# A graph network on one core: a look woven into a projection, attention's sums added a step later, and the ends of loops reordered

## The chip, the cores and the metric

The kernel runs on one core of a Trainium2 chip. The metric is the device time of one execution in microseconds (us), median of several runs. TensorE is called PE below, VectorE DVE, ScalarE ACT, GpSimd POOL and SyncE SP, as in the profile.

## What is computed

There are 3125 nodes with 256 features and 53,125 edges sorted by their destination. Two attention layers of four heads come first, then a row norm, then three relational layers, then a row norm again:

```python
# attention layer, twice
q, k, v = x@wq+bq, x@wk+bk, x@wv+bv          # 4 heads of 64
alpha = sum(q[dst]*k[src], -1)/sqrt(64)
ex = exp(alpha - segment_max(alpha, dst)[dst])
out = segment_sum(v[src]*ex/segment_sum(ex, dst)[dst], dst) + x@ws + bs
x = leaky_relu(batch_norm(out))              # over all nodes, slope 0.1
...
x = layernorm(x0 + x)
# relational layer, three times
msg = relu(x[src]*(edge_attr@nn_w.T + nn_b))
x = x@root + bias + sum_r mean_over_edges_of_type_r(msg, dst)@W[r]
...
x = layernorm(x_attention + x)
```

## The kernel before

**Tiles.** The edges are 416 tiles of 128, in 52 groups of 8. Nodes are 25 blocks of 128 for attention and 25 blocks of 126 (3 x 42) for the relational part.

**Look and first projection** (`gnn_kernel`, L171 to L359). Three rows of indices (dst, src, edge type) and x are loaded, SP issuing the rows and ACT the x pieces of eight blocks. The look turns the rows into columns, checks on the chip that the windows hold, and makes offsets and masks: some 90 small DVE instructions with small PE transposes between them. The projection takes two node blocks at a time: PE turns each block (L354), ACT copies it to `xT` (L355), PE multiplies by the keys' and values' weights (L383; four matmuls for two blocks, which the trace counts as eight), DVE adds the bias (L390, L393), SP writes to the table `kv_tab` (L396). Here a scheduler of the framework chooses the order on each engine; everywhere after it the order is that of the code. A branch on a checked flag follows.

**Attention** (`window_attention`). Each step `it` of a loop handles several groups in different stages. `rows(it+2)` has POOL issue eight indirect DMAs (L408), each gathering one tile's rows of keys and values from `kv_tab` into one of six `kvg` buffers. `queries` and `logits` (L487, L492, L494) handle group `it`; `turn` (L499) group it-1; `maxima` (L504, L505) group it-2; `weigh` (L511 to L522) forms the exponentials of group it-2 on ACT and scales its 8 x 4 value blocks by 32 ACT instructions of 65 columns; `nodes_of` (L527) makes eight one-hot tiles of group it-3 on DVE; `sums` (L534) multiplies them with the weighted values of group it-4, which frees its `kvg` buffer; `add` (L545) adds the result to an accumulator. The PSUM tile of `sums`, `pof`, has one buffer. When a block's last group has been added, `finish` divides (L564 to L567), PE adds the skip product (L572, L574), ACT moves it to `xT` (L578), DVE takes statistics (L583). The loop runs four steps past the last group, in the same order, with half the scaling on DVE (L522). `norm` then makes the batch norm's scale `sc` (L591 to L597).

**Between the layers.** After layer one, `normalise` (ACT L603, DVE L604) and the second projection alternate by two blocks (L383 again, weights of layer two), and the next gathers wait for the table. After layer two, seven steps of up to four 126-row blocks: normalise the next step's columns, `back` (PE turns a block and adds x by a second matmul with the identity, L727, L729), row statistics on DVE (L743, L744), square root on ACT (L746), reciprocal and shift on DVE (L747, L748), four scaling instructions on ACT (L751), and a write to `h_tab` (L753), from which the next gathers read.

**Relational layers** (`window_relational`). 104 half groups; POOL gathers from `h_tab` (L408, into `xsf`), PE makes edge weights (`ewf`, L824), DVE and ACT the messages (L842, L843), PE sums by one-hots (`ppf`, L850), DVE adds to a ring `kacc` three half groups later (L864). A node block, once complete, passes through `means` (DVE L878), two `turn`s (PE L889, L890; ACT L891, L893), `product` (PE L900; eight matmuls, which the trace counts as sixteen), `total` (DVE L905) and, in the last layer, `norm` (L919, L920); one of them per half group. For the last two blocks (23 and 24) what is left runs after the loop, ordered by stage: all turns first, then the products, then the totals. The next layer's gathers wait for the last write to `h_tab` (L907).

Of the kernel before, what the change touches and what calls it, by code (L numbers as in the profile page):

```python
# [8 lines left out]
F32 = mybir.dt.float32  # L9
# [15 lines left out]
H = 4  # L25
# [111 lines left out]
def gnn_kernel(ctx: ExitStack, tc: tile.TileContext, A, out):  # L137
# [33 lines left out]
    with tc.tile_pool(name="lk", bufs=1) as sp, tc.tile_pool(name="lkw", bufs=2) as wp, \  # L171
            tc.tile_pool(name="lkps", bufs=1, space=PSUM) as ps, \
            tc.tile_pool(name="lkps2", bufs=2, space=PSUM) as ps2:
        x = sp.tile([P, NT, D], F32, name="xf")
        V.memset(x[:, NT - 1, :], 0.0)
        for i in range(0, NT - 1, 8):
            S.dma_start(x[:, i:i + 8, :], A["x"][i * P:(i + 8) * P, :].rearrange("(i p) c -> p i c", p=P))
        S.dma_start(x[:NL, NT - 1, :], A["x"][(NT - 1) * P:, :])
        rows = {}
        for name in ("dst", "src", "edge_type_3"):  # L180
            t = sp.tile([RB, B, P], I32, name=name + "_r")
            if name == "dst":
                GP.iota(t[:, B - 1, :].rearrange("r (a c) -> r a c", c=32), pattern=[[1, 4], [0, 32]], base=N,
                        channel_multiplier=0)
            else:
                V.memset(t[:, B - 1, :], 0)
            a = A[name]
            n = (B - 1) * RB * P
            SY.dma_start(t[:, :B - 1, :], a[:n].rearrange("(b r c) -> r b c", b=B - 1, c=P))
            SY.dma_start(t[:TF - (B - 1) * RB, B - 1, :], a[n:TF * P].rearrange("(r c) -> r c", c=P))  # L190
            SY.dma_start(t[TF - (B - 1) * RB:, B - 1, :TR], a[TF * P:].unsqueeze(0))
            rows[name] = t
        w, bias = kv_weights(tc, A, 1, sp)

# [4 lines left out]


        d = sp.tile([RB, B, P], F32, name="d_f")
        V.tensor_copy(d, rows["dst"])
        ends = sp.tile([1, 2, T], F32, name="ends")
        for e in range(2):
            t = ps.tile([P, T], F32, name="smallps")[:1, :]
            for b in range(B):
                TE.transpose(t[:, b * RB:(b + 1) * RB], d[:, b, e * (P - 1):e * (P - 1) + 1], ident[:RB, :RB])
            V.tensor_copy(ends[:, e, :], t)
        first, last = ends[:, 0, :], ends[:, 1, :]
        halves = sp.tile([64, 2, T], F32, name="halves")  # L210
        for e in range(2):
            t = ps2.tile([P, T], F32, name="colf")
            for b in range(B):
                TE.transpose(t[:64, b * RB:(b + 1) * RB], d[:, b, e * 64:(e + 1) * 64], ident[:RB, :RB])
            V.tensor_copy(halves[:, e, :], t[:64, :])

# [3 lines left out]
        v = sp.tile([RB, B, P], F32, name="v")  # L220
        V.tensor_tensor(v[:, :, :P - 1], d[:, :, :P - 1], d[:, :, 1:], op=OP.subtract)
        V.tensor_reduce(worst[:RB, 0:1], v[:, :, :P - 1], AX.XY, OP.max)
        c = sp.tile([64, T], F32, name="c64")
        V.tensor_tensor(c, halves[:, 0, :], halves[:, 1, :], op=OP.subtract)
        V.tensor_reduce(worst[:64, 1:2], c, AX.X, OP.max)
        V.tensor_tensor(c[:, :T - 1], halves[:, 1, :T - 1], halves[:, 0, 1:], op=OP.subtract)
        V.tensor_reduce(worst[:64, 2:3], c[:, :T - 1], AX.X, OP.max)
        V.tensor_scalar(worst[:, 1:], worst[:, 1:], 1.0, None, op0=OP.add)
        wt = ps.tile([P, T], F32, name="smallps")[:3, :P]
        TE.transpose(wt, worst, ident)  # L230
        w1 = sp.tile([3, 1], F32, name="w1")
        V.tensor_reduce(w1, wt, AX.X, OP.max)
        wu = ps.tile([P, T], F32, name="smallps")[:1, :3]
        TE.transpose(wu, w1, ident[:3, :3])

        bad = sp.tile([1, 6], F32, name="bad")
        V.tensor_reduce(bad[:, 0:1], wu, AX.X, OP.max)
        r1 = sp.tile([1, T], F32, name="r1")
        for i, (tiles, width) in enumerate(((2, W2), (4, KN), (G, P))):
            n = T // tiles  # L240
            V.tensor_tensor(r1[:, :n], last[:, tiles - 1::tiles], first[:, ::tiles], op=OP.subtract)
            V.tensor_scalar(r1[:, :n], r1[:, :n], -float(width - 1), None, op0=OP.add)
            V.tensor_reduce(bad[:, 1 + i:2 + i], r1[:, :n], AX.X, OP.max)
# [4 lines left out]
        V.tensor_tensor(ahead, first[:, G::G], ahead, op=OP.subtract)  # L248
        V.tensor_reduce(bad[:, 5:6], ahead, AX.X, OP.max)
# [5 lines left out]
        V.tensor_tensor(need, need, first[:, G::G], op=OP.subtract)  # L255
        V.tensor_reduce(bad[:, 4:5], need, AX.X, OP.max)
# [3 lines left out]
        V.tensor_tensor(lim, first[:, ::2], lim, op=OP.subtract)  # L260
        b1 = sp.tile([1, 2], F32, name="b1")
        V.tensor_reduce(b1[:, 0:1], lim, AX.X, OP.max)
        V.tensor_reduce(b1[:, 1:2], bad, AX.X, OP.max)
        V.tensor_tensor(b1[:, 0:1], b1[:, 0:1], b1[:, 1:2], op=OP.max)
        V.tensor_single_scalar(flag, b1[:, 0:1], 0.0, op=OP.is_le)


        pairs = sp.tile([1, 2, T], F32, name="pairs")
        V.tensor_copy(pairs[:, 0, :].rearrange("o (a k) -> o a k", k=2), bc(first[:, ::2], 2, 2))
        V.memset(pairs[:, 1, 0:1], 0.0)  # L270
        V.tensor_tensor(pairs[:, 1, 1:], first[:, 1:], last[:, :T - 1], op=OP.is_equal)
        tr = ps.tile([P, T], F32, name="smallps")[:RB, :2 * B].rearrange("r (k b) -> r k b", k=2)
        for k in range(2):
            for b in range(B):
                TE.matmul(tr[:, k, b:b + 1], pairs[:, k, b * RB:(b + 1) * RB], ones[:1, :1], start=True, stop=True)
        per = sp.tile([RB, 2, B], F32, name="per")
        V.tensor_copy(per, tr)

        pen = sp.tile([RB, B, P], F32, name="pen")
        V.tensor_tensor(pen[:, :, 1:], d[:, :, 1:], d[:, :, :P - 1], op=OP.is_equal)  # L280
        V.tensor_copy(pen[:, :, 0], per[:, 1, :])
        V.tensor_scalar(pen, pen, -1.0, BIG, op0=OP.add, op1=OP.mult)
        SY.dma_start(pen_d[FP:FP + EP].rearrange("(b r c) -> r b c", b=B, c=P), pen)

        ld = sp.tile([RB, B, P], F32, name="ld")
        V.tensor_tensor(ld, d, bc(per[:, 0, :], 2, P), op=OP.subtract)
        SY.dma_start(ld_d.rearrange("(b r c) -> r b c", b=B, c=P), ld)
        _, dm = floor42(V, sp, d.rearrange("r b c -> r (b c)"), [RB, B * P], "d42")
        kr = sp.tile([RB, B, P], F32, name="kr")
        V.scalar_tensor_tensor(kr, rows["edge_type_3"], float(KN), dm.rearrange("r (b c) -> r b c", b=B),  # L290
                               op0=OP.mult, op1=OP.add)


        s_f = sp.tile([RB, B, P], F32, name="s_f")
        V.tensor_copy(s_f, rows["src"])
        nr = sp.tile([RB, B, P], F32, name="nr")
        V.tensor_single_scalar(rows["dst"], rows["dst"], P - 1, op=OP.bitwise_and)
        V.tensor_copy(nr, rows["dst"])
        for col, u in ((src_c, s_f), (nr_c, nr), (kr_c, kr)):
            t = ps2.tile([P, T], F32, name="colf")  # L300
            for b in range(B):
                TE.transpose(t[:, b * RB:(b + 1) * RB], u[:, b, :], ident[:RB, :RB])
            V.tensor_copy(col, t)


        pid = sp.tile([P, 1], F32, name="pid")
        GP.iota(pid, pattern=[[0, 1]], base=0, channel_multiplier=1, allow_small_or_imprecise_dtypes=True)
        V.tensor_copy(q_row, first[:, ::2])
        ni = sp.tile([1, NG], I32, name="ni")
        V.tensor_single_scalar(ni, q_row[:, ::4], 7, op=OP.logical_shift_right)  # L310
        nf = sp.tile([1, NG], F32, name="nf")
        V.tensor_copy(nf, ni)
        V.tensor_scalar(g_off, nf, float(AC), None, op0=OP.mult)
        lo = sp.tile([1, NG], F32, name="lo")
        V.scalar_tensor_tensor(lo, nf, -float(P), first[:, ::G], op0=OP.mult, op1=OP.add)
        kq, km = floor42(V, sp, first[:, ::4], [1, Q4], "n42")
        kn = sp.tile([1, 2, Q4], F32, name="kn")
        ks = sp.tile([1, 2, Q4], F32, name="ks")
        kt = sp.tile([1, 2, Q4], F32, name="kt")
        for e in range(2):  # L320
            V.tensor_scalar(kn[:, e, :], kq, float(e), None, op0=OP.add)
        V.tensor_copy(ks, kn)
        for e in range(KR, KT + 1, KR):
            V.tensor_single_scalar(kt, kn, float(e), op=OP.is_ge)
# [1315 lines left out]
```

## Time and profile before

| | us |
|---|---|
| median of 14 runs | 3019.05 (3011.58 to 3026.45) |
| the profiled execution, own time | 3022.0 |
| its span, first to last instruction | 3020.2 |
| busy: PE | 2460.8 (81%) |
| busy: DVE | 2180.2 (72%) |
| busy: POOL | 2007.2 (66%) |
| busy: ACT | 1344.9 (45%) |
| indirect DMAs issued by POOL | 832 + 1248 |

A line of the costliest groups reads: code line, engine, operation, written tile <- read tiles, count, then busy time and mean ns of one, then the idle time of its engine just before them and what ended most of it. A line of the timeline reads: start, duration, engine, line, operation, tiles, shape, count and, in brackets, the idle time before it and what ended it.

### The profile page before, as it was taken

Reading aid. Unit: us, or ns where it says so; the run is one execution under the profiler, and the core shown is the slowest. Engines: PE = TensorE matmul, PEld = TensorE weight load, DVE = VectorE, ACT = ScalarE, POOL = GpSimd, SP = SyncE. Lnnn points to the kernel's source line nnn. Section 1 sums busy time; section 2 is a strip of 40 time slices with the busy share of each in tenths; the row PEclk is TensorE's granted clock in tenths of the full one; section 3 lists DMA queues with packets and bytes.
Section 4 is the critical chain, followed back from the end, with each engine's and each line's share of the span. In section 5 each row is a group of like instructions: output and inputs, shape, how many; then the busy total and the mean of one; then the engine's idle time right before and its main releaser. Section 6 shows DMA issues by size and latency. Waiting matters only on the chain.

```text
span 3020.2 us, 45404 instructions
## 1 busy us (share of the span) xinstructions
PE 2460.8 (81%) x12358; PEld 1824.8 (60%) x12358; DVE 2180.2 (72%) x5225; ACT 1344.9 (45%) x4264; POOL 2007.2 (66%) x2093
## 2 busy tenths in 40 slices
PE   6677787867777787757989998688888878888987
PEld 3356566653566666555767776466666656666665
DVE  4599999965899999845666666466666646767775
ACT  1188878851678878743323332122222212222222
POOL 0477777722777777507777777577777757777774
PEclk8789998888799988887998999899999888999999
DMA  3788888835888888617555554444444444454443
GB/s 106 216 258 247 247 245 241 241 92 167 255 245 248 245 243 239 199 43 205 156 149 145 152 147 136 125 130 139 134 139 132 137 123 134 137 148 135 146 139 93
DMA packets 292513, 517.97 MB, mean 172 GB/s; under 512 B 102876, under 2 KB 172699, under 8 KB 292251
## 3 DMA queue, kind: packets, MB, share of 16 engines
q0 software_dynamic: 126464, 383.52, 44.7%
q1 hardware_dynamic: 162613, 128.25, 14.1%
q10 hardware_dynamic: 3174, 3.20, 0.3%
q8 instruction: 104, 1.70, 0.2%
q14 instruction: 158, 1.29, 0.1%
HBM read 468.08 MB, written 46.70 MB: 170 GB/s over the span
## 4 chain that ended last, share of the span: by engine, by line
PE 28%; DVE 10%; DMA 9%; issue 5%; POOL 2%; DVEq 1%; SPq 1%; ACT 0%; POOLq 0%; ACTq 0%
PE ppf L850 13%; DMA xsf<-h_tab,src_c 8%; PE ewf L824 8%; PE nodf L900 5%; DVE xsf L842 4%; DVE ohkf L834 2%; POOL xsf L408 2%; DVE mk L878 1%; DVE kacc L864 1%; PE nodf L889 1%; DVE xT L905 0%; SPq L788 0%; DMA abf<-in_edge_attr_dram 0%; DVEq L858 0%; PE atp L804 0%
## 5 line engine op out<-in xcount | busy, mean ns | idle before, releaser
L408 POOL DMA_INDIRECT xsf<-h_tab,src_c x1248 | 1203.9, 965 | 526.6 <-issue 183.2
L408 POOL DMA_INDIRECT kvg<-kv_tab,src_c x832 | 801.6, 963 | 357.2 <-issue 222.7
L519 ACT ACTIVATE kvg<-kvg,wts 128x65 f32<-128x65 f32 x3264 | 793.6, 335 | 3.6 <-DMA qw<-q_tab 0.2
L843 ACT ACTIVATE xsf<-xsf 128x1024 f32<-128x1024 f32 x312 | 330.0, 1058 | 1011.6 <-DVE xsf L842 1011.6
L842 DVE TENSOR_TENSOR xsf<-ewf,xsf 128x1024 f32<-128x1024 f32 x312 | 381.5, 1223 | 527.9 <-DMA xsf<-h_tab,src_c 394.2
L850 PE MATMUL ppf<-xsf,ohkf 128*126 128x256 f32 (+1 forms) x2496 | 700.4, 428 | 4.8 <-DVE kacc L864 4.8
L534 PE MATMUL pof<-kvg,ohn 128*128 128x260 f32 x1664 | 482.0, 453 | 196.4 <-ACT kvg L519 103.7
L850 PEld LDWEIGHTS ppf<-xsf,ohkf 128*126 128x126 f32 x2496 | 491.4, 207 | 187.1 <-issue 39.7
L534 PEld LDWEIGHTS pof<-kvg,ohn 128*128 128x128 f32 x1664 | 371.3, 229 | 305.5 <-ACT kvg L519 124.6
L824 PE MATMUL ewf<-nnwf,atw 33*128 33x256 f32 x2496 | 382.9, 429 | 161.9 <-DVE xsf L842 161.0
L824 PEld LDWEIGHTS ewf<-nnwf,atw 33*128 33x128 f32 x2496 | 231.2, 200 | 271.9 <-DVE xsf L842 210.9
L492 DVE TENSOR_TENSOR kvg<-qdf,kvg 128x1024 f32<-128x1024 f32 x208 | 252.1, 1212 | 67.2 <-DMA kvg<-kv_tab,src_c 46.2
L900 PE MATMUL nodf<-rwt,mts 128*126 128x256 f32 x1152 | 261.9, 380 | 1.1 <-ACT mts L893 1.1
L834 DVE TENSOR_SCALAR ohkf<-iotas,kr_c 128x126 f32<-128x126 f32 x1248 | 260.1, 295 | 0.0
L494 DVE TENSOR_REDUCE alf<-kvg 128x16 f32<-128x1024 f32 x208 | 253.8, 1220 | 7.2
L900 PEld LDWEIGHTS nodf<-rwt,mts 128*126 128x126 f32 x1152 | 218.2, 190 | 34.9 <-ACT mts L893 1.8
L487 PE MATMUL qdf<-qw,oht 32*128 32x256 f32 x1664 | 176.0, 429 | 25.9 <-DMA qw<-q_tab 16.6
L527 DVE TENSOR_SCALAR ohn<-iotas,nr_c 128x128 f32<-128x128 f32 x832 | 175.4, 298 | 0.0
L515 ACT ACTIVATE wts<-soft 128x32 f32<-128x32 f32 x104 | 20.3, 195 | 319.3 <-PE soft L513 314.6
L864 DVE SCALAR_TENSOR_TENSOR kacc<-ppf,k_high,kacc 126x256 f32 (+1 forms) x312 | 151.3, 485 | 11.1
L487 PEld LDWEIGHTS qdf<-qw,oht 32*128 32x128 f32 x1664 | 115.4, 199 | 63.8 <-DVE kvg L492 18.8
L864 DVE SCALAR_TENSOR_TENSOR kacc<-ppf,k_low,kacc 126x256 f32 (+1 forms) x312 | 148.5, 476 | 5.3 <-PE ppf L850 4.3
(213 smaller groups left out, 2005.2 us busy)
## 6 DMA issues: line engine op xcount, KB each, us to landing
atw<-at_d SPq DMA_DIRECT2D x104, 256.0 KB
xsf<-h_tab,src_c POOLq DMA_INDIRECT x1248
kvg<-kv_tab,src_c POOLq DMA_INDIRECT x832
ldb<-ld_rows SPq DMA_DIRECT2D x104, 128.0 KB
qw<-q_tab SPq DMA_DIRECT2D x416, 32.0 KB
at_d<-atw SPq DMA_DIRECT2D x52, 256.0 KB
abf<-in_edge_attr_dram SPq DMA_DIRECT2D x51, 128.0 KB
q_tab<-qs SPq DMA_DIRECT2D x50, 128.0 KB
```

The source lines that it names most:

```text
L408: return GP.indirect_dma_start(out=dst, out_offset=None, in_=table, in_offset=rows_of(idx))
L487: TE.matmul(qd[:, a, k, :], ohts[g][r, k, :], qws[g][r, :], start=True, stop=True)
L494: V.tensor_reduce(al[:, t:t + 4, :], kv.rearrange("p t (h c) -> p t h c", h=H), AX.X, OP.add)
L519: S.activation(c, c, AF.Copy, scale=w[:, j * H + q:j * H + q + 1])
L534: TE.matmul(po, oh[:, j, :], kv[:, j, D:], start=(j == 0), stop=(j == G - 1))
L824: TE.matmul(ew[:, k, a, :], ats[g][r, 2 * u + a, :], nnw[r, :], start=True, stop=True)
L834: V.tensor_scalar(oh[:, j, :], iota[:, :KM], L["kr_c"][:, g * G + j:g * G + j + 1], None, op0=OP.is_equal)
L842: V.tensor_tensor(xk, ews.pop(q), xk, op=OP.mult)
L843: S.activation(x4, x4, AF.Relu)
L850: TE.matmul(pp[:, :wide], ohs[g][:, j, :], xs[:, g % XB, j, :wide], start=(j == 4 * u), stop=(j == 4 * u + 3))
L864: V.scalar_tensor_tensor(c, pp[:, :wide], m[:KM, q:q + 1], c, op0=OP.mult, op1=OP.add)
L900: TE.matmul(q["o"], q["m"][:, c, r, :], w[:, r, c, :], start=(r + c == 0), stop=(r == R and c == 1))
```

## The change

The diff does six things, numbered as the prediction uses them.

1. **Look and first projection.** The scheduler is replaced by the code's order. The look becomes a generator `look()` of twelve portions; a step of the projection turns the next two blocks (four transposes into one tile, one ACT copy), multiplies the present two, runs one portion, then adds the bias and stores. The row loads are issued by ACT (dst first), x by SP in pieces of 2, 6, 8 and 9 blocks around the weights. The two DVE instructions for the values' bias become one; `kvs` gets three buffers.
2. **Attention's loop.** `weigh` is cut up: `less`, `weights`, and the scaling `weigh(g, a, b)`; step `it` first scales tiles 4 to 7 of group it-3, then forms the weights of it-2 and scales its tiles 0 to 3. `add` and `finish` move from group it-4 at a step's end to group it-5 at its head. `pof` moves to a pool with two buffers. A projected block of queries is added and written at the head of the next step. The accumulator is cleared by ACT instead of DVE (layer one); the norm's small vectors are loaded as rows and turned by one PE transpose.
3. **Attention's last groups.** The loop ends with the last group; what is left is written out once, with one-hots of the last three groups on POOL (after its gathers), tiles 6, 7 (then 3 to 7) scaled by one DVE instruction, and finished blocks poured through `qdf` tiles.
4. **Batch norm.** An ACT square root on a constant stands ahead of the last pour.
5. **Row norm after attention.** Normalise runs two steps ahead; x is added by DVE instead of PE; reciprocal, scaling and write of a step (`close_rows`) come one step later.
6. **Relational ends.** Blocks 23 and 24: the turns of 23 go ahead of the last half group's `products`, its product right behind them; block 24 follows, with its turns in an `ewf` tile.

```diff
-            tc.tile_pool(name="lkps2", bufs=2, space=PSUM) as ps2:
+            tc.tile_pool(name="lkps2", bufs=2, space=PSUM) as ps2, tc.manual_schedule():
...
+        rows = {"dst": load_rows("dst", S)}
+        load_nodes(0, 2)
         w, bias = kv_weights(tc, A, 1, sp)
+        load_nodes(2, 8)
+        for name in ("src", "edge_type_3"):
+            rows[name] = load_rows(name, S)
+        load_nodes(8, 16)
+        load_nodes(16, NT)
...
+        portions = look()
+        turn_nodes(*steps[0])
+        next(portions)
+        for s, (i, n) in enumerate(steps):
+            if s + 1 < len(steps):
+                turn_nodes(*steps[s + 1])
             pj = ps2.tile([P, 2, 2 * D], F32, name="pjf")
             keys_values(tc, xT, i, n, w, pj)
+            next(portions, None)
             st = wp.tile([P, 2, KV], F32, name="kvs")
             store_keys_values(tc, i, n, bias, pj, st, kv_1)
...
-            po = ps1.tile([P, AC], F32, name="pof")
+            po = qps.tile([P, AC], F32, name="pof")
...
-                V.memset(acc, 0.0)
+                S.memzero(acc)
...
-            for it in range(NG + 4):
+            for it in range(NG):
+                for f in keeps:
+                    f()
+                keeps = []
                 if it + 3 < NG:
                     loads(n, it + 3)
                 if it + 1 < NG:
                     penalties(it + 1)
                     windows(it + 1)
...
+                if it >= 5:
+                    add(it - 5)
+                while done < NT and it - 5 == last_group(done, P):
+                    ready.append(finish(done))
+                    ready[-1][0]()
+                    done += 1
+                queries(it, 1)
+                logits(it, 0)
+                if it >= 4:
                     sums(it - 4)
+                if it >= 2:
                     maxima(it - 2)
+                if it >= 1:
                     turn(it - 1)
+                logits(it, 1)
+                if it >= 2:
+                    less(it - 2)
+                if it >= 3:
+                    weigh(it - 3, 4, G)
+                if it >= 2:
+                    weights(it - 2)
+                    weigh(it - 2, 0, 4)
+                if it >= 3:
                     nodes_of(it - 3)
...
+            nodes_of(z - 2, GP)
+            sums(z - 3)
+            maxima(z - 1)
+            turn(z)
+            less(z - 1)
+            weigh(z - 2, 4, 6)
+            weigh_rest(z - 2, 6)
+            weights(z - 1)
+            close(z - 4)
+            nodes_of(z - 1, GP)
...
+            sums(z - 2)
+            maxima(z)
+            less(z)
+            weigh(z - 1, 0, 3)
+            weigh_rest(z - 1, 3)
+            weights(z)
+            nodes_of(z, GP)
+            close(z - 3)
+            pour()
+            sums(z - 1)
+            weigh(z, 0, 3)
+            weigh_rest(z, 3)
+            close(z - 2)
+            pour()
+            sums(z)
+            close(z - 1)
+            close(z)
+            S.activation(sc[:, 0, 0:1], L["eps"], AF.Sqrt)
+            pour()
...
-                TE.matmul(t[:KM, u, c * P:(c + 1) * P], xT[:, c, (i + u) * KM:(i + u + 1) * KM], ident,
-                          start=True, stop=False)
-                TE.matmul(t[:KM, u, c * P:(c + 1) * P], ident[:KM, :KM],
-                          xrs[(i + u) // 16][:, (i + u) % 16, c * P:(c + 1) * P], start=False, stop=True)
+                TE.transpose(t[:KM, u, c * P:(c + 1) * P], xT[:, c, (i + u) * KM:(i + u + 1) * KM], ident)
...
+            if s + 2 < len(steps):
+                j, k = steps[s + 2]
+                normalise(sc, j * KM, (j + k) * KM)
+            if s + 1 < len(steps):
+                after = back(*steps[s + 1])
+            y = xrs[i // 16][:, i % 16:i % 16 + m, :]
+            V.tensor_tensor(y, t[:KM, :m, :], y, op=OP.add)
+            for u in range(m):
+                st = sp.tile([KM, 6], F32, name="lnst")
+                V.bn_stats(st, y[:, u, :])
+                V.bn_aggr(mv[:, i + u, :], st)
+            S.activation(rs[:, 0, i:i + m], mv[:, i:i + m, 1], AF.Sqrt, bias=L["eps"][:KM])
+            if s:
+                close_rows(*steps[s - 1])
...
+                for f in late[:1]:
+                    f[1](), f[2]()
                 if s >= 2:
                     products(n, s - 2)
+                for f in late[:1]:
+                    f[3]()
...
+            before, last = late
+            before[4](), last[1](), last[2](), last[3]()
```

In `close(g)`, `add(g)` is followed by the divisions of the blocks that it completes; `pour()` runs the skip product on PE and the copy on ACT for all completed blocks.

## Prediction

> **What bounds the kernel now.** The page first: DVE, PE and POOL are busy 72, 81 and 66%, so no engine bounds the whole. The slices and POOL's two groups say why.
>
> ```profile
> span 3020.2 us, 45404 instructions
> ...
> POOL 0477777722777777507777777577777757777774
> ...
> L408 POOL DMA_INDIRECT xsf<-h_tab,src_c x1248 | 1203.9, 965 | 526.6 <-issue 183.2
> L408 POOL DMA_INDIRECT kvg<-kv_tab,src_c x832 | 801.6, 963 | 357.2 <-issue 222.7
> ```
>
> POOL shows five level stretches with holes between. Its seven tenths are full: a gather takes 0.95 us and the next starts 0.30 later, so 1.255 each. The view of line L408 gives the holes:
>
> ```profile
> its engine sat idle before it (us, times) until:
>   issue: 405.9, 1324
>   DMA h_tab<-kvg: 101.0, 1
>   DMA q_tab<-qs: 100.7, 1
>   PE ppf L850: 95.4, 313
>   DMA h_tab<-xT: 46.1, 2
> ```
>
> The long ones are single: 101.0 and 100.7 us behind the attention layers, 46.1 for two behind the relational layers. The first gather starts at 102.58, the last ends at 2989.3, 30.9 before the end. 102.6+100.7+101.0+46.1+30.9 = 381 us; the other 2639 are five times 416 gathers at POOL's pace (416 x 1.255 = 522, measured 526 to 529). So **inside the loops nothing but a stalled POOL counts, and only the 381 us of ends can be won.** By the timeline, the hole behind attention one (the last gather ends at 631.48) is 48.6 us until the norm's scale at 680.1, then 52.1 of projection:
>
> ```profile
> 637.55 7.77 ACT L519 ACTIVATE kvg<-kvg,wts 128x65 f32<-128x65 f32 x32
> 639.68 3.75 PE L534 MATMUL pof<-kvg,ohn 128*128 128x260 f32 x16 [2.40 <-ACT kvg L519]
> 649.47 6.66 PE L534 MATMUL pof<-kvg,ohn 128*128 128x260 f32 x16 [3.70 <-ACT kvg L519]
> 660.90 6.07 PE L534 MATMUL pof<-kvg,ohn 128*128 128x260 f32 x16 [4.30 <-ACT kvg L519]
> 668.15 3.72 PE L534 MATMUL pof<-kvg,ohn 128*128 128x260 f32 x16
> ```
>
> The four last sums are about ten apart, each waiting for ACT's scaling. Behind attention two it is 50.0 to the scale (1308.83), then 51.0 of row norm.
>
> **The change part by part** (own time of the profiled execution 3022.0, 3 above the median; every part is a difference, so it carries over).
>
> *Part 1, the first projection: -20.5.* Before, PE's first projection matmul is at 27.4, because x's second piece and dst land late (the first full ACT copy is at 24.3, dst's cast at 23.3), and the last ends at 98.2; the gather follows 4.4 later. In those 71 us, the tile view of `pjf` shows 100 matmuls starting 0.43 apart, 43 us; the transposes wait 19.8 for ACT's copies (one PSUM tile), and PE stands 33.2 to 45.7 for a store behind the look's DVE work. After, a step turns the next two blocks while ACT's copy is covered by the present matmuls: 43 + 50 transposes at 0.22 = 11, + the look's own PE work of about 6 = 60 us. DVE's list of the look is 31 us (portions of 0.6 to 5.8), the stores 13 x 1.5: 51 in all, under PE's 60, with two `pjf` tiles to even out the portions: I add 3 for collisions. The start: dst goes first, but ACT issues nine row loads ahead of its first copy. On SP the same kind of loads held the queue from 0.8 to 12.5 (two single ones for 3.86 and 4.66), so ACT is free at 9 to 14, plus its table load of 1.28; I take 14.5. 14.5+60+3+4.4 = 82 against 102.6. Ends: start at 8 with no collisions, 72 (-30); DVE and PE in turn as far as they are now, 15+71+4.4 = 90 (-12).
>
> *Part 2, the loop: 0.* What it must keep is the buffer: the gathers of group g+6 wait for the sums of g. Between the end of those sums and that gather there were 3 to 9 us in both layers, once 0.3 (group 2). The split puts half of a group's scaling into the next step, but in front of the wait for `less`, where ACT had 319.3 us of idle time (page: wts), so the group's scaling ends some 0.6 to 1 us later than now (one 0.6 copy more ahead of it); on the other side the sums no longer wait for `add` (two `pof` buffers). DVE's work per step is unchanged (69.5 of each 75 us). Moved q writes still precede SP's loads of `qw`, which are three steps ahead. Clearing the accumulator on ACT (7.92 us for 126x9252, so 5.8) takes 5.7 off DVE, both beside gathers already running; the vectors' transpose and copy, 0.4, too. If the cover goes, each group pays: see the rivals.
>
> *Part 3, attention's end, twice: -10 and -10.5.* After, the chain is PE's. From the last gather's end: landing 2.9, last logits 2.4, one-hots of group 48 on DVE 1.65, four sums at 3.72 = 14.9, `turn` and two `less` 1.75, two skip products 2.3, last `add` 1.0, two divisions 1.6, skip, copy and statistics of the last block 2.9, aggregate 1.5, square root to scale 1.3: 34.2. ACT's share per group is 12 scalings, 2.9, beside PE; DVE's five tiles in one instruction (0.36 each) 1.8. That is 14 and 16 less than 48.6 and 50.0. But three of the four sums took 5.3 to 6.7 now, partly for a slow clock (0.70 granted in 1350 to 1425, another thin stretch) rather than for ACT; with half of that excess, 38.5 and 39.5. Ends: 34 and 43, so 6 to 15 won per layer. The one-hots on POOL have no row: the nearest is its 128x128 affine select, 0.28, which makes 2.3 per group, hidden; the far one is a gather's 1.26. One-hots of 51 wait for the sums of 49 (two buffers), so above 0.72 us each they stand in front of the last sums; at 1.26 a layer loses 8.7. I take 0.35.
>
> The Trainium skill (SBUF — State Buffer, section Who interferes with whom) speaks against this: a DVE instruction with two SBUF inputs contends with a GpSimd instruction that reads SBUF, the later one blocking. The `weigh_rest` multiply is such a one; by the rule, as an estimate from the 1.8, some 4 us a layer would be added. No row here shows a POOL operation of this kind beside DVE.
>
> *Part 4:* a table load of 1.28 now lies beside the aggregate (1.51) and cost nothing: 0.
>
> *Part 5, the row norm: -1.7.* Now a round of four blocks takes 7.03:
>
> ```profile
> 1335.00 1.50 ACT L603 ACTIVATE xT<-xT,sc 128x504 f32<-128x504 f32 x2
> 1335.85 1.38 DVE L604 SCALAR_TENSOR_TENSOR xT<-xT 128x504 f32<-128x504 f32 x2 [2.75 <-ACT xT L603]
> ...
> 1339.41 0.30 ACT L746 ACTIVATE rsl<-mvl,epss 126x4 f32<-126x4 f32 x1 [2.91 <-DVE mvl L744]
> 1339.75 0.18 DVE L747 RECIPROCAL rsl<-rsl 126x4 f32<-126x4 f32 x1 [0.37 <-ACT rsl L746]
> 1340.22 1.93 ACT L751 ACTIVATE kvg<-qdf,rsl 126x256 f32<-126x256 f32 x4 [0.51 <-DVE rsl L748]
> 1342.03 1.51 ACT L603 ACTIVATE xT<-xT,sc 128x504 f32<-128x504 f32 x2
> ```
>
> The reader sees ACT and DVE in turn. Normalising two steps ahead doesn't part them: ACT's order is normalise(s+2), root(s), scaling(s-1), then normalise(s+3), and scaling(s-1) waits for DVE's reciprocal behind step s's statistics. A full round is 0.85 (ACT ahead of DVE) + 1.38 + 1.22 (the new add; row L492) + 2.15 (statistics) + 0.4 + 1.9 (scaling) = 7.9, longer than now. Won is at the ends: two normalises stand done at 1312.4, step 0 has no scaling, steps 5 and 6 no normalise. Step by step DVE ends statistics at 1317.3, 1323.2, 1331.0, 1338.8, 1345.6, 1349.2, 1350.5; ACT then scales step 5 to 1353.7 and 6 to 1354.2, and the last write goes out at 1354.7 against 1356.4. Ends: DVE alone (5.15 a round) -8.6; scaling slower from SBUF than from PSUM, +2.
>
> *Part 6, relational ends: -0.4 each, -1.2.* Before, the products of blocks 23 and 24 run last, 3.6 each:
>
> ```profile
> 1902.74 3.72 PE L900 MATMUL nodf<-rwt,mts 128*126 128x256 f32 x16 [0.35 <-ACT mts L893]
> 1906.29 3.62 PE L900 MATMUL ppf<-rwt,mts 128*126 128x256 f32 x16
> ```
>
> After, product 23 comes earlier, but the turns of 23 (1.3, waiting for its means at 1897.3) hold the last half group's products by 1.7; means of 24 end at 1902.7, product 23 at 1903.9, the turns at 1905.2, product 24 at 1909.2 to 1909.9 against 1909.9. Ends: 0 and -0.8 each; +1 if ACT's copies come late.
>
> **Sum:** -20.5-20.5-1.7-1.2 = -44: 2978 for this execution, **2975** by the median 3019.
>
> **The rivals.**
> - *POOL one-hots late.* At 0.9 to 1.26 us each, or held up by `weigh_rest` (two groups a layer, 1.8 each, 3.6): 1.5 to 9 per layer given back, 2985 by the middle. For: there is no row; an indirect DMA takes POOL 0.95. Against: affine select 0.28, iota 0.24.
> - *The first projection gains half.* Row loads hold ACT longer and portions collide: first gather at 90 to 93, so 2984.
> - *The row norm runs at DVE's pace, and the sums at 3.72 in both tails:* 2975-7-8 = 2960.
> - *The ring stalls, and it is slower.* If in the new order ACT's step (0.6+7.77+0.2+0.3 of work) kept its waits in series, sums of g would come later than the slack of 3 to 9 us, POOL would wait each group, and 0.43 us per group over 104 groups eat the 44. A step of 10.9 instead of 10.04 costs 90: 3065. Against: the wait is slack, and `weights` now waits behind four scalings.
> - *The ends aren't what counts:* the gathers would start earlier but stall later. The gaps inside a layer sum to 2.0 to 2.9 us over POOL's pace, so there is nothing to give back: 2.
>
> **How the numbers follow.** Forecast 0.60, POOL late 0.12, projection half 0.13, the low case 0.07, ring 0.05, nothing 0.03. Leaving out the ring and nothing, the cases' bounds run from 2955 (all low ends together are unlikely) to 2995: the range. A measurement of this kernel tells about 0.2%, 6 us. Faster 0.92, same 0.03, slower 0.05.
>
> **What would show it.** First gather near 82 us; holes of POOL of 90 and 89 behind the attention layers, 23 behind the relational ones, and level stretches of 526 between. Wrong would be: gaps among gathers above 0.3 us inside a layer (part 2), POOL one-hots ending after `pof` of group 50 (part 3), ACT copying its first block after 16 us (part 1), a round of the row norm at 5 us (part 5).

## The result, and the profile after

The changed kernel takes **2978.4 us** (median of 6 runs, 2976.3 to 2980.8) against 3019.1 (28 runs): ratio 0.9865, 95% interval 0.9854 to 0.9876, 40.7 us less. The prediction said 2975. The profiled execution took 2973.31, 48.7 less than that of before. The page of after, the same four lines:

```profile
span 2971.5 us, 45205 instructions
...
POOL 0677777744777777627777776677777757777774
...
L442 POOL DMA_INDIRECT xsf<-h_tab,src_c x1248 | 1198.3, 960 | 487.2 <-issue 207.8
L442 POOL DMA_INDIRECT kvg<-kv_tab,src_c x832 | 796.1, 957 | 321.2 <-issue 223.6
```

The gathers are as many as before, and their idle time has gone from 526.6 and 357.2 to 487.2 and 321.2. The first comes at 88.33 instead of 102.58. By the starts and ends of POOL's gathers, in us, one profile each, after against before (all sums of this document that go by stretch are made in this way; "scale" is the end of the last DVE instruction that forms the norm's scale `sc`, and a "tail" is the time from a layer's last gather to it):

| | before | after | difference | predicted |
|---|---|---|---|---|
| first gather | 102.6 | 88.3 | -14.2 | -20.5 |
| five stretches of 416 gathers | 2639.0 | 2626.6 | -12.4 | 0 |
| attention one: last gather to scale, scale to gather | 48.6 + 52.1 | 37.1 + 52.0 | -11.7 | -10 |
| attention two: the same | 50.0 + 51.0 | 40.1 + 49.7 | -11.2 | -10.5 - 1.7 |
| relational holes and end | 23.5, 22.6, 30.9 | 23.1, 22.9, 31.9 | +0.9 | -1.2 |

The timeline of after behind attention one, the four last sums (start, us, then the idle time before them and what ended it):

```profile
619.47 5.32 PE L575 MATMUL pof<-kvg,ohn 128*128 128x260 f32 x16 [4.13 <-ACT kvg L558]
625.52 3.77 PE L575 MATMUL pof<-kvg,ohn 128*128 128x260 f32 x16
631.14 3.67 PE L575 MATMUL pof<-kvg,ohn 128*128 128x260 f32 x16
635.99 3.67 PE L575 MATMUL pof<-kvg,ohn 128*128 128x260 f32 x16
```

They follow one another at 5 to 6 us instead of ten, and only before the first does PE stand idle. A round of the row norm in the same view:

```profile
1290.84 1.49 ACT L647 ACTIVATE xT<-xT,sc 128x504 f32<-128x504 f32 x2
1291.67 1.38 DVE L648 SCALAR_TENSOR_TENSOR xT<-xT 128x504 f32<-128x504 f32 x2 [2.84 <-ACT xT L647]
...
1296.48 0.30 ACT L861 ACTIVATE rsl<-mvl,epss 126x4 f32<-126x4 f32 x1 [4.15 <-DVE mvl L860]
...
1296.74 2.07 ACT L839 ACTIVATE kvg<-kvg,rsl 126x256 f32<-126x256 f32 x4
```

The next L647 starts at 1298.72, 7.88 later: DVE still waits 2.84 for ACT, ACT 4.15 for DVE. The two last products behind the first relational layer:

```profile
1855.31 3.62 PE L1015 MATMUL nodf<-rwt,mts 128*126 128x256 f32 x16
1860.63 3.62 PE L1015 MATMUL ppf<-rwt,mts 128*126 128x256 f32 x16
```

The first is earlier, but between the two stand the turns of the last block, and the second ends 19.9 after the last gather (1844.33) as it did before (1909.91 after 1889.59: 20.3). And the start:

```profile
4.55 4.05 ACTq L194 DMA_DIRECT2D dst_r<-in_dst_dram  x1
...
17.42 0.43 DVE L236 CAST d_f<-dst_r 104x512 f32<-104x512 int32 x1 [13.74 <-DMA dst_r<-in_dst_dram]
...
22.99 0.59 ACT L380 COPY xT<-xtps 128x512 f32<-128x512 f32 x1
```

ACT issues nine loads of index rows; the last of each three, 1x5 numbers, holds it for 4.05, 7.22 and 3.14 us. dst is cast at 17.4, and ACT copies its first turned block at 23.0, where I had 14.5 for the start.

### The profile page after: what moved, and what is told of

It reads as the page before. It is cut to its first block, busy times and chain, and to the rows that moved or that the text cites. A ratio compares the mean times of both kernels' runs of the same rounds, so it can differ in the third digit from the quotient of the medians.

```text
span 2971.5 us, 45205 instructions
## 1 busy us (share of the span) xinstructions
PE 2463.6 (83%) x12210; PEld 1816.5 (61%) x12210; DVE 2181.8 (73%) x5151; ACT 1344.9 (45%) x4223; POOL 2030.5 (68%) x2141
## 3 DMA queue, kind: packets, MB, share of 16 engines
q0 software_dynamic: 126464, 383.52, 45.3%
## 5 line engine op out<-in xcount | busy, mean ns | idle before, releaser
L442 POOL DMA_INDIRECT xsf<-h_tab,src_c x1248 | 1198.3, 960 | 487.2 <-issue 207.8
L442 POOL DMA_INDIRECT kvg<-kv_tab,src_c x832 | 796.1, 957 | 321.2 <-issue 223.6
L575 PE MATMUL pof<-kvg,ohn 128*128 128x260 f32 x1664 | 439.3, 422 | 11.7 <-ACT kvg L558 8.5
L575 PEld LDWEIGHTS pof<-kvg,ohn 128*128 128x128 f32 x1664 | 341.4, 211 | 112.3 <-ACT kvg L558 29.5
L520 PE MATMUL qdf<-qw,oht 32*128 32x256 f32 x1664 | 204.3, 517 | 21.7 <-DMA qw<-q_tab 15.7
L532 PE MATMUL soft<-identf,alf 128*32 128x128 f32 x312 | 59.3, 304 | 163.3 <-DVE fmax L537 158.2
L520 PEld LDWEIGHTS qdf<-qw,oht 32*128 32x128 f32 x1664 | 130.5, 246 | 66.3 <-issue 33.3
L568 DVE TENSOR_SCALAR ohn<-iotas,nr_c 128x128 f32<-128x128 f32 x784 | 166.8, 302 | 0.0
L975 DVE SCALAR_TENSOR_TENSOR kacc<-ppf,k_low,kacc 126x256 f32 (+1 forms) x312 | 148.5, 476 | 10.5 <-PE ppf L961 9.8
```

Source lines behind the costliest of these rows:

```text
L442: return GP.indirect_dma_start(out=dst, out_offset=None, in_=table, in_offset=rows_of(idx))
L520: TE.matmul(qd[:, a, k, :], ohts[g][r, k, :], qws[g][r, :], start=True, stop=True)
L575: TE.matmul(po, oh[:, j, :], kv[:, j, D:], start=(j == 0), stop=(j == G - 1))
L975: V.scalar_tensor_tensor(c, pp[:, :wide], m[:KM, q:q + 1], c, op0=OP.mult, op1=OP.add)
```

## The experiments

The first four kernels ran on a chip on which before itself took 3676.5 us (17 runs); in the four profiles from there the gathers stall inside the layers (last section). After itself was not run there, so these four ratios are not to be set beside its 0.9865; I use them among themselves, and the stages outside the gathers' stretches. The others ran on chips where before took 3020.4 and 3016.8.

**Part 1 alone** (`p1_only`): before, with the loads, `look` and first projection of after.

> The kernel before with part 1 alone (loads, look and first projection of after; loop, tails, norms of before). If the parts add up and part 1 is worth what the profile of after shows: first gather at 88 us instead of 102.6, the rest as before, 14 less: 3005 us, ratio 0.995. The rival is that the five stretches of gathers, 11.6 us shorter in the profile of after, got shorter by part 2 of the change: then they stand at 526 to 529 here as before. If it is the pace of POOL in one execution, they may differ here too, with nothing in the loop changed.

Measured: 3668.5, ratio 0.9971 (0.9947 to 0.9995); first gather 88.06. What part 1 gives to the first gather is what after showed, 14. The first two stretches, 666.2 and 665.3, belong to the last section; with the stalls they can't tell whether part 2 shortens the stretches.

**The small loads issued by POOL** (`rows_pool`), and **the 103 rows cut** (`rows_split`):

```
-            engine.dma_start(t[:TF - (B - 1) * RB, B - 1, :], ...)
-            engine.dma_start(t[TF - (B - 1) * RB:, B - 1, :TR], ...)
+            GP.dma_start(...)        # rows_pool: both
+            engine.dma_start(...)    # rows_split: rows 0 to 95, rows 96 to 102, and the 1x5
```

> After with the two small loads of each index list (103 rows, 1x5) issued by POOL instead of ACT. If ACT, held by these issues until 21.7, sets the start of the first projection: the first copy of a turned block at 5 to 8 us, first gather at 72 to 76. If the landing of dst's 103 rows does (DVE's cast at 17.4, and PE's look transposes stand ahead of the first projection step): first step at 17 to 18 instead of 24.3, first gather at 81 to 82, 6 less: 2972 us. If neither does, 88 as in after.

> After with each load of 103 rows cut in 96 and 7 rows, on ACT as in after. If the 103 rows trickle in because their number doesn't divide, and the 1x5 issue behind them waits for that: dst's cast at 8 to 10 us, ACT's issues of 1x5 below 1 us instead of 4.05, 7.22 and 3.14, first gather at 75 to 79: 2968 us. If ACT's issues wait for something else (the queue's length, any small load): the cast earlier, but ACT's first copy at 20 to 23 still, first gather at 85 to 88: 2976 to 2978.

Measured: `rows_pool` 0.982 (0.9787 to 0.9852), first gather 77.78, where I expected 72 to 76 or 81 to 82; `rows_split` 0.9813 (0.9779 to 0.9847), first gather 86.49. The two ratios can't be told apart; the stages tell the difference. Timeline of `rows_pool`:

```profile
2.32 0.56 POOL L194 DMA_DIRECT2D dst_r<-in_dst_dram  x1
...
5.84 0.59 ACT L380 COPY xT<-xtps 128x512 f32<-128x512 f32 x1 [2.27 <-PE xtps L379]
...
10.00 0.43 DVE L236 CAST d_f<-dst_r 104x512 f32<-104x512 int32 x1 [6.32 <-DMA dst_r<-in_dst_dram]
...
14.39 4.56 PE L418 MATMUL pjf<-wkv,xT 128*128 128x512 f32 x8
```

POOL gets rid of the same load in 0.56, ACT copies at 5.84, and the projection starts at 14.4: what holds it now is dst's landing (cast at 10.0) and the look's PE work behind the cast. In `rows_split` dst's cast comes at 13.5, 3.9 earlier than in after, but ACT is held until 19.3 and copies at 20.6: 1.8 won. So in after ACT, held by its own DMA issues, sets the start. Of what I expected of the cut, one half came true: the issues of 1x5 fell to 0.29, 0.23 and 0.23; but ACT then stood between its issues, 3.9 us ahead of src's last.

**ACT's half of the row norm a step earlier** (`norm_ahead`):

```
             if s + 2 < len(steps):
-                normalise(sc, j * KM, (j + k) * KM)
+                normalise(sc, j * KM, (j + k) * KM, "v")     # DVE's half
+            if s + 3 < len(steps):
+                normalise(sc, ..., "s")                       # ACT's half of the step after
```

> After with ACT's half of the row norm's normalise issued one more step ahead, so that it stands before the square root and the scaling of the step before and not behind them; DVE's half stays where it is. If the round of 7.88 is ACT and DVE in turn: a round of DVE's own work, 5.2, four to five full rounds, the hole behind attention two from 89.8 to 77 to 80, 10 to 12 less: 2967 us. The rival, that DVE or the writes of h_tab set the round anyway: 7.9 still, and 2978.

Measured: 0.9805 (0.9773 to 0.9838); from scale to gather 39.6 instead of 50.2 in `rows_pool` and `rows_split`, and 49.7 in after.

```profile
1540.82 1.27 DVE L650 SCALAR_TENSOR_TENSOR xT<-xT 128x504 f32<-128x504 f32 x2
...
1542.92 1.49 ACT L648 ACTIVATE xT<-xT,sc 128x504 f32<-128x504 f32 x2
...
1545.65 1.27 DVE L650 SCALAR_TENSOR_TENSOR xT<-xT 128x504 f32<-128x504 f32 x2
```

A round is 4.83 now, DVE starts L650 without waiting, and ACT's L648 lies inside DVE's statistics.

**The plain end** (`tail_plain`): the last groups in the order of the loop, not in the one written out by hand; one-hots on DVE.

```
-            for it in range(NG):
+            for it in range(NG + 5):          # with guards; weigh_rest(it - 3, 4) once it >= NG
...
-            nodes_of(z - 2, GP)               # and all of the written order up to close(z)
```

> After with part 3 undone: the new loop is simply run five steps on for the last groups, as before ran four, with ACT and DVE sharing the last scalings as before; projection, norms and relational layers as in after. If the reordered tail is worth what the profile showed (last gather's end to the norm's scale 37.1 and 40.1 against 48.6 and 50.0): 48 to 52 here again, some 22 more than after. The rival, that the tails got shorter because the loop hands over less work (part 2): 40 to 43 here, 3 to 8 more. On a chip where the gathers are not the pace of the loop, the two stretches must be told by the tails alone.

Measured: 2978.0, ratio 0.9867 (0.9852 to 0.9882), as after. From the last gather to the scale 34.2 and 38.3 against after's 37.1 and 40.1. One profile tells a tail to some 2 us: `best` (below), with the same plain end, has 36.1 and 39.6. Neither is anywhere near 48 to 52, so my theory of part 3 falls: the written order is not what shortened the tails. Something that the loop brings did.

**One more PSUM buffer in before** (`pof_two`), and **one less in the plain end** (`plain_one_pof`). The trace of before, read again for the adds:

```profile
639.10 0.49 DVE L545 SCALAR_TENSOR_TENSOR accf<-pof,g_high,accf 128x260 f32 x1
...
648.88 0.49 DVE L545 SCALAR_TENSOR_TENSOR accf<-pof,g_high,accf 128x260 f32 x1
...
660.32 0.49 DVE L545 SCALAR_TENSOR_TENSOR accf<-pof,g_high,accf 128x260 f32 x1
```

They end at 639.59, 649.37 and 660.81; the sums of the next group start at 639.68, 649.47 and 660.90 (the lines in the prediction), each 0.09 to 0.10 later. The trace names ACT's scaling, but by the order of the code a group is scaled two steps ahead of its sums: the scalings that these three need had ended at 633.40, 645.32 (637.55 + 7.77) and 649.37 (645.43 + 3.94), 4 us and more ahead of the start. What the add stands behind, on DVE, are the eight one-hots of the very group that waits:

```profile
637.01 1.65 DVE L527 TENSOR_SCALAR ohn<-iotas,nr_c 128x128 f32<-128x128 f32 x8
...
646.80 1.65 DVE L527 TENSOR_SCALAR ohn<-iotas,nr_c 128x128 f32<-128x128 f32 x8
...
658.23 1.65 DVE L527 TENSOR_SCALAR ohn<-iotas,nr_c 128x128 f32<-128x128 f32 x8
```

From the first one-hot to the sums it is 2.67 each time. Layer two shows the same: adds end at 1269.43, 1280.09 and 1290.21, and the next sums start at 1269.53, 1280.19 and 1290.31.

```
-            po = ps1.tile([P, AC], F32, name="pof")
+            po = qps.tile([P, AC], F32, name="pof")     # two buffers; plain_one_pof: the reverse
```

To make room for the second buffer, `pof_two` also gives up the tile `nodeps` and puts one skip product behind the loop into a query tile.

> The kernel before with one thing changed: two PSUM buffers for a group's sums (pof) instead of one; the block that finishes beside the last one takes a query tile. In before each of the last sums starts 0.1 us after the add of the group before has ended (639.59, 649.37, 660.81 against 639.68, 649.47, 660.90), though the trace names ACT. If that one buffer is what made the tails long: 48.6 and 50.0 fall to 38 to 43, 14 to 22 less in all, ratio 0.993 to 0.995. If the sums wait for ACT's scaling, as I read it in the prediction, or if the add must come a step later as well: 46 to 50, ratio 0.998 to 1.

> The kernel with the plain end (new loop run five steps on) with one PSUM buffer for the sums instead of two, add still a step later. If adding a step later is enough to take the add out of the sums' way: tails of 34 to 40 as with two buffers (34.2 and 38.3), ratio 0.987. If the second buffer is needed: 42 to 50, ratio 0.990 to 0.994, and perhaps stalls among the gathers.

Measured, from the last gather to the scale, layer one and two:

| | add in the sums' own step | add a step later |
|---|---|---|
| one `pof` | 48.6, 50.0 (before) | 38.0, 44.6 (`plain_one_pof`) |
| two `pof` | 38.8, 42.5 (`pof_two`) | 34.2, 38.3 (`tail_plain`) |

`plain_one_pof` took 2982.6, ratio 0.9885 (0.9868 to 0.9903), and `pof_two` 3000.1, 0.994 (0.9926 to 0.9954). The last sums of `pof_two` in its timeline:

```profile
641.67 1.65 DVE L526 TENSOR_SCALAR ohn<-iotas,nr_c 128x128 f32<-128x128 f32 x8
642.05 3.74 PE L533 MATMUL pof<-kvg,ohn 128*128 128x260 f32 x16 [0.48 <-issue]
...
647.90 1.65 DVE L526 TENSOR_SCALAR ohn<-iotas,nr_c 128x128 f32<-128x128 f32 x8
...
648.28 5.43 PE L533 MATMUL pof<-kvg,ohn 128*128 128x260 f32 x16 [2.01 <-ACT kvg L518]
...
654.89 3.67 PE L533 MATMUL pof<-kvg,ohn 128*128 128x260 f32 x16
```

They start 6 to 7 us apart instead of ten, and 0.38 after the group's first one-hot instead of 2.67. The buffer alone gives 17.3 of the 21.4 that after won in the tails; the later place of the add alone gives 16.0. With one buffer and the later place the sums still start 0.10 after an add (in `plain_one_pof` at 614.99, 623.92 and 636.36), but that add no longer stands behind their own one-hots. Both changes together give 26.1 by `tail_plain` and 22.9 by `best`, so whichever comes second brings 6 to 10 more. (The right column also has the scaling split in two steps and DVE's share in one instruction; these were not tried alone.)

**POOL's one-hots twice** (`pool_twice`) and **on DVE** (`tail_dve`).

```
+                for _ in range(1 if engine is V else 2):            # pool_twice
                     engine.tensor_scalar(oh[:, j, :], iota, ...)
-            nodes_of(z - 2, GP)                                     # tail_dve, three times
+            nodes_of(z - 2)
```

> After with each one-hot of the two tails made twice on POOL, the second over the first. A one-hot took 0.58 us, so a pair takes 1.16, over the 0.72 from which I reckoned that the last sums wait for them. If so: the 24 pairs of a tail take 28 us instead of 23 between the first and the last with the waits of now, the last sums start behind the last pair, and each tail grows by 3 to 10 us, 6 to 20 in all: ratio to before 0.989 to 0.993. If POOL has more room than I reckoned: below 2 in each tail.

> After with the tails' one-hots on DVE (0.2 each) instead of POOL (0.58 to 0.77 each). If POOL, slower than I took it and held up beside DVE's two-input multiply, sets the end of the last sums: tails of 34 to 36 and 37 to 39 instead of 37.1 and 40.1, 2 to 5 less in all. If DVE, with 1.65 us more per group, sets it: 2 to 4 more per tail. If PE does: the same within 1.

Measured: `pool_twice` 3003.2, 0.9946 (0.9932 to 0.996), tails 45.3 and 51.6, 8.2 and 11.5 longer; `tail_dve` 2980.4, 0.988 (0.9863 to 0.9898), tails 38.0 and 41.2, 1 longer each, which two profiles can't tell from nothing. In after, POOL's share by the tile view (ns min/median/max):

```profile
L568 POOL TENSOR_SCALAR ohn<-iotas,nr_c x24: 590/596/2430, 614.3 to 636.7; 128x128 f32<-128x128 f32 x24
```

A one-hot takes 0.60, near my decision point of 0.72, and doubled they do set the end. The prediction's own reckoning (8.7 a layer at 1.26, so 16 one-hots beyond 0.72) gives 7.7 for pairs of 1.2, less than the 8.2 and 11.5 measured; the pairs that ran beside DVE's multiply were longer, up to 2.9, and are not in that reckoning. Single, the one-hots are hidden, and DVE would have hidden them as well.

**The relational layers of before** (`rel_old`): part 6 undone.

> After with part 6 undone, the relational layers of before. I had put the new ends at -0.4 each; the profile of after showed holes of 23.1 and 22.9 against 23.46 and 22.61 and a last end 0.9 longer. If the reordering is worth nothing: holes of 22.6 to 23.5, the end 30.9, within 1 us of after, which the measurement can't tell. If it is worth more than one profile shows, over 2 us.

Measured: 2978.6, 0.9865 (0.985 to 0.9881), the time of after; holes 25.5 and 23.4, end 30.7. Sum of the three 79.6 against 77.9 in after and 77.0 in before: nothing that could be told.

**Together** (`rows_norm`: POOL's loads, the cut and the earlier normalise, on after; `best`: POOL's loads and the earlier normalise on the plain end, and `next(portions)` ahead of the first projection step left out, so that the look's portions come a step later).

> After with both finds together: the small row loads issued by POOL, the 103 rows cut in 96 and 7, and ACT's half of the normalise a step earlier. POOL's loads alone brought the first gather to 77.8, the earlier normalise the distance from scale to gather from 49.7 to 39.7. If they add up: first gather at 74 to 78, hole behind attention two at 79 to 81, 20 less than after, ratio to before 0.980 on a chip as that of after's profile. If the cut gives nothing beyond POOL's issue, the first gather stays at 77.8; if it does, DVE's cast comes at 6 to 8 instead of 10.0.

> The plain end, the small row loads issued by POOL, ACT's half of the normalise a step earlier, and the first portion of the look moved behind the first projection step, so that PE's first step doesn't wait for DVE's cast of dst (10.0). If each does what it did alone: first gather at 73 to 76 (77.8 less up to 4), tails 34 to 39, hole behind attention two 78 to 80: 2952 to 2957, ratio to before 0.978 to 0.9795. If the look's DVE work, now a step later, sets the end of the projection: first gather at 78 again, 2957 to 2960.

Measured: `rows_norm` 2959.6, 0.9804 (0.979 to 0.9817), first gather 78.84, scale to gather 40.1; the two finds add up, and the cut gives nothing that could be told (cast at 9.63 against 10.00, first gather no earlier than in `rows_pool`). `best` 2955.5, **0.9792** (0.9776 to 0.9808), first gather 78.48: PE's first step begins at 13.31, for now x's second piece lands at 12.4, and the step's gain is lost again in the stage behind it (65.2 to the gather instead of 63.4). It beats before and after; against `rows_norm`, which ran on another chip, the intervals overlap.

## Why the prediction was right, and where it was not

- **The frame held.** On the two chips where before took 3016.8 to 3020.4, the gains and losses of every kernel lie outside the gathers' stretches, but for the 9 us below: the gaps among a layer's gathers beyond POOL's 0.30 sum to 1.9 to 2.9 us, and once to 4.1 (`tail_plain`) and 3.5 (`plain_one_pof`).
- **Part 1, mis-sized: -14.2, not -20.5.** The failing step is "ACT is free at 9 to 14", taken from SP's issues of the same loads: ACT was free at 21.7. It is the second rival (90 to 93) in cause, and nearly in time. ACT's first copy came 8.5 late (23.0 for 14.5), but from that copy to the gather it took 65.3, less than my 60 + 3 + 4.4 = 67.4. From PE's first projection matmul it is 63.8 in after and 63.4 in `rows_pool`, which at a start of 14.4 came out at 77.8.
- **Part 3, the right size for a wrong reason.** I put -20.5 to the written order and measured -21.4; but my reading "each waiting for ACT's scaling" was the failing step. The sums waited for the one `pof` buffer, that is for an add that stood behind DVE's one-hots. I had named the buffer in part 2 and costed it at 0, looking only at the loop, where the wait is slack. The size was luck as well: half the excess of the long sums is 2.65 in layer one (6.66 and 6.07 against 3.72) and 2.6 in layer two (5.55, 5.34 and 5.40), which on top of 34.2 makes 36.8 twice, not the 38.5 and 39.5 that I wrote.
- **Part 3, POOL.** 0.60 against my 0.35, still below the 0.72 from which I reckoned that it counts; `pool_twice`, above that point, lengthens both tails. My sign of being wrong did come up: POOL's last one-hot ended at 637.3, behind the sums of group 50 (631.14 + 3.67 = 634.81), and it cost nothing to be seen. The rule that I weighed (the Trainium skill, SBUF — State Buffer, section Who interferes with whom) holds in that the two engines did contend: beside `weigh_rest` (627.10 to 628.57, and 630.04 to 631.55) one-hots took 2.43 and 1.84, the same to 0.01 in both layers. But it was POOL that waited both times, also where its one-hot had begun 0.48 before the multiply; "the later one blocking" is not what the trace shows there. DVE's multiplies took 1.47 and 1.51. That is 1.8 and 1.2 of POOL's time per layer, and by `tail_dve` it cost the tail nothing that could be told.
- **Part 5: right.** A round of 7.88 (7.9 predicted) and -1.3 (-1.7); `norm_ahead` confirms that the turn-taking, not DVE, made the round.
- **Parts 4 and 6.** The table load is hidden, at 636.8, in front of the last copies. Part 6 is 0.9 worse in one profile and not to be told from 0.
- **Part 2, 0 expected: no stalls, but not nothing.** The five stretches sum to 2626.6 to 2632.0 in the eight profiles with the new loop, leaving out the chip with the stalls, and to 2639.0 and 2637.1 in the two with the old one (before, `pof_two`): some 9 us. It isn't the chip: `pof_two` ran on the same one as three of the eight. The mean gather is 0.959 to 0.961 against 0.964. But `rel_old`, with the relational layers of before, has 1577.7 in these layers, where before has 1583.5; so there it isn't the work beside the gathers. Nor does a run tie it to the loop, for the eight also have parts 1, 4 and 5. What makes it stays open.

So the sum, -44 for -40.7, was right in part by luck. In the two profiles it is -48.6: against my terms, part 1 fell 6.3 short and part 6 2.1, and the stretches gave 12.4 that I hadn't seen. (By the medians the gain is 8 less than by the profiles, because after's profiled execution is 5 below its median and before's 3 above.) Of my four signs of being wrong, two came up: ACT copied its first block after 16 us, which is the miss of part 1, and POOL's one-hots ended late, which was harmless.

## What to carry to other kernels

A wait that the trace puts to one engine may be for a buffer that another frees: before reordering a tail, look at what ended within 0.1 us of each start, and try one more PSUM buffer, which here gave 17.3 us in the tails of before, where the whole of after gave 21.4. Loads that are issued by an engine with work of its own are work of that engine; in a start-up, small and oddly shaped loads go to one that is idle. When two engines take turns in a loop, moving work a step ahead helps only if it is issued before the instruction that waits for the other engine.

## What the runs showed of the hardware

- Issuing a load of 20 bytes held ACT for 4.05, 7.22 and 3.14 us, and POOL for 0.51 to 0.56. With the 103 rows ahead of it cut in two it held ACT for 0.23 to 0.29, but ACT then stood between its issues. The uncut 103 rows arrived at 13 to 16 packets per us, where some 200 packets of the 104x3 load came in one us. The Trainium skill (DMA: Bandwidth & Descriptors, Why a DMA increments its semaphore by 16 and not by 1) says that a transfer uses the largest number of engines up to 16 that divides its outermost count. The trace agrees: by that rule 104 goes to 13 engines and 103, a prime, to one, and 200 / 13 is 15 packets per us and engine.
- On one chip of those used, SP's loads starved beside the gathers. The DMA view of 35 us in the first attention layer (packets, MB, share), `rows_pool` there and after on its own chip:

```profile
q0 software_dynamic: 2244, 7.42, 74.9%
q1 hardware_dynamic: 511, 0.40, 4.0%
```

```profile
q0 software_dynamic: 2145, 7.09, 69.0%
q1 hardware_dynamic: 2411, 2.09, 20.4%
```

The gathers (q0) move as much in both, SP's queue (q1) a fifth. SP's issues of `qw` then last up to 14.3 us for four in the first steps of the loop, the logits wait, and gathers stall 33 to 37 us behind the ring's first six groups and 2 to 3 us in most groups after. The granted clock was 0.81 to 0.82 there and 0.87 to 0.89 on the others; whether that is cause or effect, and why this chip differs, wasn't settled. There the loop does matter: the attention stretches are 666.2 and 665.3 in `p1_only`, with the old loop, and 649.1 to 655.1 in the three kernels with the new one.
